# First image of an attention kernel's first phase: seven products for part of q and k and all of v, an early power on GpSimd, and a later place for the weights' sums

## The chip, the core and the metric

The kernel runs on one core of a Trainium2 chip. A core has TensorE (matmuls; PE in the profile, its weight loads PEld), VectorE (DVE), ScalarE (ACT), GpSimd (POOL) and SyncE (SP), each with its own queue of instructions that it takes in order. SP and ACT also start DMAs. Engines wait for one another through semaphores. Matmuls write to PSUM, of which there are eight banks; the other working memory is SBUF. The metric is the device time of one execution in microseconds (us), lower being better.

## The reference

Two attention layers run one after the other over x of shape (8, 512, 32, 32): eight images of 512 channels and 1024 tokens, in float32.

```python
# layer 0
h = group_norm(xf, gn_w, gn_b)                      # 32 groups of 16 channels, over all tokens
qkv = jnp.einsum('oc,bct->bot', qkv_w, h) + qkv_b[None, :, None]
qkv = qkv.reshape(b * NUM_HEADS, -1, T)             # 8 heads of 64 channels
q, k, v = jnp.split(qkv, 3, axis=1)
q = fake_quant(q); k = fake_quant(k); v = fake_quant(v)   # 8 bits, from the min and max of the whole tensor
w = softmax(jnp.einsum('bct,bcs->bts', q * scale, k * scale))
a = jnp.einsum('bts,bcs->bct', w, v)
x = xf + jnp.einsum('oc,bct->bot', proj_w, a) + proj_b[None, :, None]
# layer 1: group norm, one head of 512 channels, no quantization
x = x + proj(softmax(q k^T / sqrt(512)) v)
```

The minimum and maximum that `fake_quant` needs are taken over all eight images. So no score can be computed before q, k and v of all images are known.

## The kernel before

**Phases.** Phase 1 computes the norm and q, k and v of layer 0 for all images, keeps their running minima and maxima, and writes q, k and v to DRAM. It ends about 624 us into the span, where the next products (`fold`) start. Then the extremes are reduced over the core (a `partition_all_reduce` on GpSimd), and a long second phase reads q, k and v back, quantizes them, and does the attention of both layers. The change touches phase 1 alone, and in it the first image, image 0.

**How a product is tiled.** An image is a tile x of 128 partitions by 4 chunks of channels (cc) by 1024 tokens. Its norm is done in place. A q or k tile is 128 channels (two heads, j = 0 to 3) by 1024 tokens. Computed directly it takes two accumulators of 512 tokens with four matmuls each, one for each chunk (lines 643 to 646; matmuls are all recorded under line 192, the helper `mm`). A float32 matmul shows in the trace as two records.

**Seven products.** For images 1 to 7 q, k and v are computed by a scheme of the Strassen-Winograd kind: the product of 2 by 2 blocks takes seven block products rather than eight, at the cost of sums of blocks of the weights (`weight_sums`, once) and of the tokens (`token_sums`, for each image), and of extra additions when accumulators are read. `qk_block(b, j)` computes the q tile j and the k tile j together; `v_block(b, n)` computes a quarter of the tokens of each half for v. Each is a generator that stops after each of its seven products, and a caller takes turns between them. In a block, two accumulators x and y are written, read by VectorE or ScalarE, and written on: between two products into the same accumulator there is a reading that TensorE must wait for. Image 0 is computed directly, eight q and k tiles and eight v tiles, and the weights' sums are made meanwhile.

**Image 0.** Its norm is done chunk by chunk (`norm(0, CC)`), as the chunks of x arrive: statistics on VectorE, an average over groups by two tiny matmuls (`gps_a`, the second from `gd_a`), an addition on VectorE, the inverse square root as a power of -0.5 on GpSimd (line 246), and the scaling of the chunk on VectorE, in two halves of 512 tokens. The matmuls of the first two tiles (`early`) follow each chunk as it is ready. A library that the power needs is loaded by an instruction that stands in GpSimd's queue right behind the three `memset`s of lines 169 to 173. The constant part of each bias (`bias(i)`) comes from TensorE too: `wt`, then `wc` or `wr`.

**What sets the order.** The kernel is written in an order, and a scheduling layer puts the instructions of each engine in a sequence by priority and readiness; only the matmuls are chained to one another (in `mm`). The listing of the built program shows the result: on VectorE, the weights' sums (`wa` and `room`), which in the text come after image 0's norm, stand in the middle of the last chunk's norm, between its `gd_a` steps. On TensorE that chunk's `gps_a` stands ahead of one matmul of chunk 1 and four of chunk 2. The generators `ahead` (norm and sums of image 1) and `more` (the weights' sums) are advanced by hand between tiles.

**Buffers that matter.** Phase 1 has eight PSUM banks, three x buffers (so image 3 is loaded when image 0 is no longer read), four buffers for q and k tiles, three for v, and one each for the token sums of even and odd images.

Of the kernel before, what the change touches and what calls it, by code (L numbers as in the profile page):

```python
# [9 lines left out]
F32 = mybir.dt.float32  # L10
# [4 lines left out]
ALU = mybir.AluOpType  # L15
AX = mybir.AxisListType

P = 128
B, C, HH, WW = 8, 512, 32, 32
T = HH * WW  # L20
CC = C // P
NT = T // P
NH = T // 512
HEADS = 8
PAIRS = HEADS // 2
# [17 lines left out]
IN_ORDER = mybir.DependencyInfo(mybir.DependencyClass.NoSync, mybir.DependencyReason.DATA)  # L43
# [10 lines left out]
def attn_pair_kernel(  # L54
# [9 lines left out]
    nc = tc.nc  # L64
    PSUM = bass.MemoryType.PSUM

    class InOrder:
# [5 lines left out]

        def __init__(self, engine):
            self.engine, self.last, self.t, self.chores = engine, None, 0.0, []

        def __getattr__(self, name):
            op = getattr(self.engine, name)

            def call(*args, **kw):  # L80
                ins = op(*args, **kw).ins  # L81
                if InOrder.planned:
                    if name == "dma_start":
                        self.t = max(self.t, pe.t) + 0.5
                    if self.last is not None:
                        tc.add_manual_dep(ins, self.last.name, IN_ORDER, reason="order")
                    self.last = ins

            return call
# [52 lines left out]
    dve, act, pe = InOrder(nc.vector), InOrder(nc.scalar), InOrder(nc.tensor)  # L142
# [15 lines left out]
    const = ctx.enter_context(tc.tile_pool(name="const", bufs=1))  # L158
# [9 lines left out]
    fourth = const.tile([P, P], F32, name="fourth")  # L168
# [2 lines left out]
    nc.gpsimd.memset(ones16, 1.0)  # L171
    mhalf = const.tile([P, CC], F32, name="mhalf")
    nc.gpsimd.memset(mhalf, -0.5)


    gavg = const.tile([P, P], F32, name="gavg")
# [14 lines left out]
    def mm(ps, lhsT, rhs, **kw):  # L191
        ins = nc.tensor.matmul(ps, lhsT=lhsT, rhs=rhs, **kw).ins  # L192
        part = lhsT.shape[-1] / P if lhsT.shape[-1] in (32, 64) else 1.0
        if rhs.dtype in (BF, F16):
            part *= 0.25 * lhsT.shape[0] / P
        pe.t += math.prod(rhs.shape[1:]) * 1.677e-3 * part
        if last_mm[0] is not None:
            tc.add_manual_dep(ins, last_mm[0].name, IN_ORDER, reason="order")
        last_mm[0] = ins
# [71 lines left out]
    v_d = [dram.tile([P, NT, C], F32, tag=f"v{b}", name=f"v_d{b}") for b in range(B)]  # L271
# [8 lines left out]
    with ExitStack() as fast:  # L280
# [39 lines left out]
        cut, at = {}, 0  # L320
        for name, n in (
            ("qmax", N_MAX), ("kmax", N_MAX), ("vmax", NT * B), ("qmin", B * PAIRS),
            ("kmin", B * PAIRS), ("vmin", NT + (B - 1) * NT // 2),
        ):
            cut[name] = rcs[:, at : at + n]
            at += n
        qmax, kmax, vmax, qmin, kmin, vmin = cut.values()
# [37 lines left out]
        with tc.tile_pool(name="p1w", bufs=1) as p1w, tc.tile_pool(name="p1", bufs=3) as p1, tc.tile_pool(  # L365
            name="p1o", bufs=4
        ) as p1o, tc.tile_pool(name="ps_1", bufs=8, space=PSUM) as ps_1:

            def one(name):
                return ps_1.tile([P, 512], F32, tag="b", name=name)  # L370

            wqkv = p1w.tile([P, CC, 3 * C], F32, name="wqkv")
            wn = {}
            xs, hs, cs = {}, {}, {}
            col = {n: 0 for n in ("qmax", "kmax", "vmax", "vmin")}

            def column(name, tile_):
                col[name] += 1
                return tile_[:, col[name] - 1 : col[name]]
# [37 lines left out]
                for i in range(3)  # L417
            ] + [room[:, 4:6, :]]

            def weight_sums():  # L420
                tt = dve.tensor_tensor
                (a11, a12), (a21, a22) = (
                    [wqkv[:, k, bass.ts(i, C)] for k in (K0, K1)] for i in (0, 1)
                )
                tt(ss[0], a21, a22, ALU.add)
                yield
                tt(ss[1], ss[0], a11, ALU.subtract)
                yield
                tt(ss[2], a11, a21, ALU.subtract)
                yield  # L430
                tt(ss[3], a12, ss[1], ALU.subtract)
                yield
                (w11, w12), (w21, w22) = (
                    [wqkv[:, k, 2 * C + i * C // 2 : 2 * C + (i + 1) * C // 2] for i in (0, 1)]
                    for k in (K0, K1)
                )
                tt(vs[:, 0], w11, w12, ALU.subtract)
                yield
                tt(vs[:, 1], w22, vs[:, 0], ALU.subtract)
                yield  # L440
                tt(vs[:, 2], w22, w12, ALU.add)
                yield
                tt(vs[:, 3], w21, vs[:, 1], ALU.subtract)
                yield

            def quarters(b):
                h = hs[b]
                return [h[:, k, bass.ts(hf, 512)] for k in (K0, K1) for hf in range(NH)]

            def token_sums(b):  # L450
                a, b_, c, d = quarters(b)
                cs[b] = t = l1p.tile(
                    [P, 4, CC // 2, 512], F32, tag="hv"[b % 2], name=f"sums_{b}"
                )
                tt = dve.tensor_tensor
                tt(t[:, 0], b_, a, ALU.subtract)
                yield
                tt(t[:, 1], d, t[:, 0], ALU.subtract)
                yield
                tt(t[:, 2], d, b_, ALU.subtract)  # L460
                yield
                tt(t[:, 3], c, t[:, 1], ALU.subtract)
                yield
# [122 lines left out]
            vb = p1w.tile([P, 2, C], F32, name="vb")  # L586
# [37 lines left out]
            bq, bk, bv = (bias(i) for i in range(3))  # L624
            then = iter((part[1], part[2], part[2], part[3], part[3]))
            for cc in range(CC):
                for t in range(2):
                    for hf in range(NH):
                        qk_mm(0, early[t], t, hf, cc)
                        if (cc, hf) in ((0, 1), (1, 0), (1, 1)):  # L630
                            next(next(then, iter(())), None)
                if cc >= 2:
                    next(bq, None)
            load_x(2)
            ahead = prepare(1)
            more = weight_sums()
            hn = hs[0]
            for t in range(2 * PAIRS):
                isk, j = divmod(t, PAIRS)
                if t < 2:  # L640
                    ps = early[t]
                else:
                    ps = [one(f"qkps_0_{t}_{hf}") for hf in range(NH)]
                    for hf in range(NH):
                        for cc in range(CC):
                            qk_mm(0, ps, t, hf, cc)
                if t >= PAIRS - 1:
                    next(bk, None)
                if t == 2 * PAIRS - 1:
                    next(bv)  # L650
                qk = p1o.tile([P, T], F32, tag="qk", name=f"qk1_0_{t}")
                mx, mn = (kmax, kmin) if isk else (qmax, qmin)
                for hf in range(NH):
                    dve.tensor_scalar(
                        qk[:, bass.ts(hf, 512)], ps[hf], qkb[:, t : t + 1], None,
                        ALU.add, ALU.max, accum_out=column("kmax" if isk else "qmax", mx),
                    )
                dve.tensor_reduce(mn[:, j : j + 1], qk, AX.X, ALU.min)
                nc.sync.dma_start((k_d if isk else q_d)[0][j], qk)
                if t > 0:  # L660
                    next(ahead, None)
            for t in range(NT):
                ps = one(f"vps_0_{t}")
                for cc in range(CC):
                    mm(
                        ps,
                        lhsT=hn[:, cc, bass.ts(t, P)],
                        rhs=wqkv[:, cc, 2 * C : 3 * C],
                        start=(cc == 0),
                        stop=(cc == CC - 1),  # L670
                    )
                next(bv, None)
                vt = p1o.tile([P, 2, C], F32, tag="v2", bufs=3, name=f"v1_0_{t}")[:, 0, :]
                dve.tensor_add(vt, ps, vb[:, 0, :])
                dve.tensor_reduce(column("vmax", vmax), vt, AX.X, ALU.max)
                dve.tensor_reduce(column("vmin", vmin), vt, AX.X, ALU.min)
                nc.sync.dma_start(v_d[0][:, t, :], vt)
                next(ahead, None)
                next(more, None)
            for rest in (ahead, more):  # L680
                for _ in rest:
                    pass


            TURNS = (0, 0, 2, 0, 0, 2, 0, 2, 0, 0, 2, 1, 1, 2, 1, 1, 2, 1, 2, 1, 1)
            for b in range(1, B):
# [4 lines left out]
                ahead = prepare(b + 1) if b + 1 < B else iter(())  # L691
                for n in range(2):
                    blocks = (qk_block(b, 2 * n), qk_block(b, 2 * n + 1), v_block(b, n))
# [307 lines left out]
        xts, sums, wms, wps, mvs = {}, {}, {}, {}, {}  # L1001
# [62 lines left out]
        tt = dve.tensor_tensor  # L1064
# [924 lines left out]
```

## Time and profile before

| | us |
|---|---|
| median of 3 runs | 2689.42 |
| lowest and highest | 2688.77, 2689.55 |
| the profiled execution | 2690.02 |
| its span | 2688.2 |
| granted TensorE clock over the span | 0.99 |
| first matmul of q | at 14.40 |
| end of image 0's products | at 112.52 |
| end of image 1's products | at 185.6 |

Starts are counted from the span's start. "Busy" is the time in which an engine worked on instructions; the chain of waits is followed back from the last instruction, at each step to what released it. Of DMA, 10 MB arrive in the first 30 us (x of images 0 to 2 and the weights), at about 400 GB/s from 14 us on.

### The profile page before, as it was taken

The page shows a single profiled execution, that of the slowest core. Times are in us where ns is not written, and L with a number is a line of the kernel's source. Part 1 is how long each engine was busy: PE and PEld are TensorE (multiplying, and loading weights), DVE is VectorE, ACT ScalarE, POOL GpSimd, SP SyncE. Part 2 cuts the span into 40 slices and gives each one's busy share as a digit, 9 for nine tenths or more (in the row PEclk, how much of TensorE's full clock was granted, in tenths as well). Part 3 has the DMA queues.
Part 4 walks back from the last instruction along what each step waited for, and adds up shares of the span by engine and source line. Part 5 has one row for each costly group of instructions (what it writes and reads, how often), then busy time and mean ns, then how long its engine had stood idle before and what let it go on. Part 6 is the DMA issues. An engine that isn't in the chain of part 4 may idle for free.

```text
span 2688.2 us, 33380 instructions
## 1 busy us (share of the span) xinstructions
PE 2594.8 (97%) x13110; PEld 1657.8 (62%) x13110; DVE 1904.8 (71%) x2749; ACT 1259.0 (47%) x1582; POOL 201.7 (8%) x156
## 2 busy tenths in 40 slices
PE   7999999998779999999999999999999999999998
PEld 3455555553225774776577567757765775677687
DVE  6666666647997776876777687678767776876544
ACT  0011111114875665666476556646664765565021
POOL 0000000000220000100100010001001000100000
PEclk9999999998999999999999999999999999999999
DMA  5323223224421123212322321233133223212311
GB/s 196 113 110 125 101 96 117 94 113 146 134 64 40 56 68 118 95 56 94 111 64 71 107 87 56 79 109 94 56 95 110 64 76 103 87 40 69 112 36 37
DMA packets 147464, 241.97 MB, mean 90 GB/s; under 512 B 26592, under 2 KB 92128, under 8 KB 145760
## 3 DMA queue, kind: packets, MB, share of 16 engines
q1 hardware_dynamic: 116448, 181.50, 20.1%
q10 hardware_dynamic: 30848, 58.23, 6.3%
q8 instruction: 105, 1.72, 0.3%
q14 instruction: 63, 0.52, 0.1%
HBM read 152.86 MB, written 86.28 MB: 89 GB/s over the span
## 4 chain that ended last, share of the span: by engine, by line
PE 78%; DVE 9%; issue 7%; DMA 2%; ACT 2%; POOL 1%; SPq 0%; ACTq 0%; DVEq 0%; POOLq 0%
PE s L192 15%; PE o L192 13%; PE qkps L192 10%; PE pj L192 8%; PE av L192 7%; PE v2ps L192 7%; PE g L192 5%; PE vps L192 5%; PE st L192 4%; PE sm L192 4%; DVE two L81 2%; ACT pt L81 1%; DVE sums L81 1%; DVE x L81 1%; DVE h L81 1%
## 5 line engine op out<-in xcount | busy, mean ns | idle before, releaser
L81 DVE TENSOR_TENSOR two<-pt,two 128x1024 f16<-128x1024 f32 x512 | 618.1, 1225 | 165.9 <-POOL two L873 134.7
L81 ACT ACTIVATE pt<-st,esc 128x1024 f32<-128x1024 f32 x512 | 543.5, 1115 | 371.0 <-PE st L192 348.1
L81 ACT CAST two<-pt 128x1024 f16<-128x1024 f32 x364 | 369.5, 1055 | 7.8 <-ACT p L81 5.1
L873 POOL CAST two<-pt 128x1024 f16<-128x1024 f32 x128 | 177.1, 1384 | 1585.5 <-PE sm L192 1376.4
L81 ACT ACTIVATE u<-qkps,qkb 128x512 f32<-128x512 f32 x84 | 57.7, 687 | 476.5 <-PE qkps L192 472.1
L192 PE MATMUL av<-two,v 128*64 128x512 f16 x2048 | 255.3, 387 | 0.6
L192 PE MATMUL s<-g,h 128*128 128x256 f32 x1024 | 234.2, 381 | 0.0
L192 PE MATMUL pj<-ao,wp 128*128 128x512 f32 x512 | 223.9, 595 | 1.5 <-DVE ao L81 1.5
L192 PEld LDWEIGHTS s<-g,h 128*128 128x128 f32 x1024 | 192.9, 190 | 31.8 <-issue 4.3
L192 PE MATMUL st<-q,k 64*128 64x512 bf16 x1024 | 166.5, 386 | 42.3 <-ACT pt L81 35.6
L192 PEld LDWEIGHTS <-v 128*64 128x64 f16 x2048 | 104.1, 110 | 133.1 <-issue 62.0
L192 PE MATMUL s<-g,sums 128*128 128x256 f32 x768 | 178.4, 381 | 0.2 <-DVE p L81 0.2
L192 PE MATMUL o<-p,v 128*128 128x256 f32 x768 | 175.2, 382 | 0.0
L192 PEld LDWEIGHTS pj<-ao,wp 128*128 128x128 f32 x512 | 96.1, 190 | 123.1 <-issue 112.9
L192 PE MATMUL qkps<-x,wqkv 128*128 128x512 f32 x352 | 163.5, 608 | 1.8 <-DVE x L81 1.8
L192 PEld LDWEIGHTS o<-p,v 128*128 128x128 f32 x768 | 144.3, 190 | 25.6 <-issue 6.9
L192 PEld LDWEIGHTS s<-g,sums 128*128 128x128 f32 x768 | 144.7, 190 | 24.2 <-issue 4.6
L192 PE MATMUL qkps<-sums,wa 128*128 128x512 f32 x336 | 153.3, 592 | 0.0
L192 PE MATMUL sm<-two,ones 128*32 128x512 f16 x2048 | 141.6, 386 | 1.3 <-ACT rs L81 1.3
L192 PEld LDWEIGHTS <-k 64*128 64x128 bf16 x1024 | 36.6, 94 | 165.6 <-issue 163.1
L192 PE MATMUL o<-g,vsum 128*128 128x256 f32 x512 | 125.4, 401 | 11.5 <-DVE g L81 11.5
L192 PE MATMUL g<-h,wa 128*128 128x256 f32 x512 | 122.1, 387 | 2.5 <-DVE h L81 2.5
(193 smaller groups left out, 3504.8 us busy)
## 6 DMA issues: line engine op xcount, KB each, us to landing
rs<-rs_d SPq DMA_DIRECT2D x80, 256.0 KB
x<-in_x_dram SPq DMA_DIRECT2D x32, 512.0 KB
raw<-q_d SPq DMA_DIRECT2D x32, 512.0 KB
raw<-k_d SPq DMA_DIRECT2D x32, 512.0 KB
raw<-v_d SPq DMA_DIRECT2D x32, 512.0 KB
x_d<-h SPq DMA_DIRECT2D x64, 256.0 KB
x<-x_d ACTq DMA_DIRECT2D x64, 256.0 KB
out_dram<-x SPq DMA_DIRECT2D x64, 256.0 KB
```

Of the source, the lines that this page charges most:

```text
L81: ins = op(*args, **kw).ins
L192: ins = nc.tensor.matmul(ps, lhsT=lhsT, rhs=rhs, **kw).ins
L873: copy(two[:, 0], pt)
```

## The change

Four things are done.

- In image 0 the q and k tiles 0 and 1 are still computed directly (`for t in (0, 1, PAIRS, PAIRS + 1)`). The tiles 2 and 3 of q and k and all of v come from two rounds of a `qk_block` and a `v_block` taking turns, seven products each. The token sums of image 0 are made as well, and the order in which they and the weights' sums are advanced is written out.
- On GpSimd a power of constants, whose result nobody reads, stands behind the memsets. The library's load, which was followed by the first norm's power, now stands ahead of this one.
- Every sum of weights and of image 0's tokens is made to follow, on VectorE, the last instruction of the last chunk's norm (`tt_behind`, `dve.after(normed)`). This is an order only: both are on the same engine, and no semaphore is added.
- The biases of k and v are advanced earlier, and the columns of v's minima are counted anew.

```diff
 class InOrder
             self.engine, self.last, self.t, self.chores = engine, None, 0.0, []
+            self.latest = None
+
+        def after(self, ins):
+
+            tc.add_manual_dep(self.latest, ins.name, IN_ORDER, reason="order")
...
-                ins = op(*args, **kw).ins
+                ins = self.latest = op(*args, **kw).ins
...
     nc.gpsimd.memset(mhalf, -0.5)
+
+    nc.gpsimd.tensor_tensor(
+        const.tile([P, 1], F32, name="first_pow"), fourth[:, 0:1], mhalf[:, 0:1], ALU.pow
+    )
...
-            ("kmin", B * PAIRS), ("vmin", NT + (B - 1) * NT // 2),
+            ("kmin", B * PAIRS), ("vmin", B * NT // 2),
...
+            def tt_behind(*args):
+                dve.tensor_tensor(*args)
+                dve.after(normed)
+
             def weight_sums():
-                tt = dve.tensor_tensor
+                tt = tt_behind
...
 def token_sums(b)
-                tt = dve.tensor_tensor
+                tt = dve.tensor_tensor if b else tt_behind
...
                             next(next(then, iter(())), None)
+                            normed = dve.latest
...
             ahead = prepare(1)
-            more = weight_sums()
-            hn = hs[0]
-            for t in range(2 * PAIRS):
+            more, sums = weight_sums(), token_sums(0)
+
+            more = iter([more, more, sums, sums, more, more, more, more, sums, sums, more, more])
+            for t in (0, 1, PAIRS, PAIRS + 1):
...
-                if t >= PAIRS - 1:
+                if t == 1:
+                    next(bk)
+                elif t == PAIRS:
                     next(bk, None)
-                if t == 2 * PAIRS - 1:
                     next(bv)
+                elif t == PAIRS + 1:
+                    next(bv, None)
...
-                if t > 0:
-                    next(ahead, None)
-            for t in range(NT):
-                ps = one(f"vps_0_{t}")
-                for cc in range(CC):
-                    mm(
-                        ps,
-                        lhsT=hn[:, cc, bass.ts(t, P)],
-                        rhs=wqkv[:, cc, 2 * C : 3 * C],
-                        start=(cc == 0),
-                        stop=(cc == CC - 1),
-                    )
-                next(bv, None)
-                vt = p1o.tile([P, 2, C], F32, tag="v2", bufs=3, name=f"v1_0_{t}")[:, 0, :]
-                dve.tensor_add(vt, ps, vb[:, 0, :])
-                dve.tensor_reduce(column("vmax", vmax), vt, AX.X, ALU.max)
-                dve.tensor_reduce(column("vmin", vmin), vt, AX.X, ALU.min)
-                nc.sync.dma_start(v_d[0][:, t, :], vt)
-                next(ahead, None)
-                next(more, None)
-            for rest in (ahead, more):
-                for _ in rest:
-                    pass
+                for g in (next(more, None) for _ in range(2)):
+                    next(g)
+            for n in range(2):
+                blocks = (qk_block(0, 2 + n), v_block(0, n))
+                for i in range(14):
+                    next(blocks[i % 2])
+                    next(next(more, iter(())), None)
+                    if i % 2 == 1:
+                        next(ahead, None)
+            for _ in ahead:
+                pass
+            del hs[0], cs[0]
```

In the listing of the changed program, VectorE has the whole norm of the last chunk without a gap and then the sums of weights and tokens in turns; TensorE has k's tiles 0 and 1 behind q's, with the three biases between them, and then the 28 products; all instructions from image 1's first evictions on stand as before.

## The prediction, made before the changed kernel had run

> **What bounds the kernel now.** I read the page first, then the chain of waits over the first 180 us, then the busy time by stretches, then GpSimd's instructions in order of time.
>
> The page's first part says that TensorE is the bound:
> ```profile
> PE 2594.8 (97%) x13110; PEld 1657.8 (62%) x13110; DVE 1904.8 (71%) x2749; ACT 1259.0 (47%) x1582; POOL 201.7 (8%) x156
> ```
> The table by stretches (length, then busy PE, PEld, DVE, ACT, POOL, granted clock, DMA share, GB/s) says how full it is around the change. The first image's products end at 112.52 us:
> ```profile
> 28.00:30.00 2.00, 2.00 (x5) 0.80 (x4) 1.56 (x5) 0.00 (x0) 0.93 (x1) 0.68 0.56 219
> 30.00:32.00 2.00, 2.00 (x4) 0.91 (x3) 2.00 (x4) 0.00 (x0) 0.00 (x0) 0.50 0.00 0
> ...
> 36.00:112.52 76.52, 76.52 (x205) 34.29 (x204) 52.36 (x102) 1.17 (x2) 1.02 (x1) 1.00 0.25 96
> 112.52:185.60 73.08, 72.92 (x230) 42.91 (x229) 48.22 (x96) 8.24 (x12) 1.01 (x1) 1.00 0.28 106
> ```
> From 36 us on TensorE has no gap, while VectorE is busy 52 of 76 us: work taken from TensorE there moves everything after it. At 28 to 32 us TensorE looks full, but its clock was 0.68 and 0.50. The chain (start, length, what) shows what comes before that:
> ```profile
> 12.98 0.60 POOL grstd_a L246
> ...
> 13.60 0.16 DVE grstd_a L81
> ...
> 14.40 3.78 PE qkps L192 x4
> ...
> 24.81 1.05 issue
> 25.86 0.15 DVE gd_a L81
> 26.01 1.14 DVE wa L81
> 27.15 0.08 DVE gd_a L81
> 27.23 0.04 issue
> 27.27 0.38 PE gps_a L192 x2
> 27.65 6.10 PE qkps L192 x10
> ```
> Two 128x1024 sums of weights (wa; the "issue" of 1.05 us covers the first) stand on VectorE between the small steps (gd_a) of the last chunk's norm. TensorE, whose order puts that chunk's second average (gps_a) ahead of ten ready records, waits for it from 24.67 to 27.27. Then those ten records take 6.10 us.
>
> GpSimd and the step that releases it, from the order of time:
> ```profile
> 8.69 0.16 DVE L81 TENSOR_SCALAR grstd_a<-gps_a 128x1 f32<-128x1 f32 x1 [0.68 <-PE gps_a L192]
> 12.98 0.59 POOL L246 TENSOR_TENSOR grstd_a<-grstd_a,mhalf 128x1 f32<-128x1 f32 x1 [11.96 <-DVE gmv_a L81]
> 18.68 0.55 POOL L246 TENSOR_TENSOR grstd_a<-grstd_a,mhalf 128x1 f32<-128x1 f32 x1 [5.11 <-DVE grstd_a L81]
> ...
> 823.18 1.04 POOL L873 CAST two<-pt 128x1024 f16<-128x1024 f32 x1 [17.42 <-PE sm L192]
> 831.89 1.05 POOL L246 TENSOR_TENSOR grstd_b<-grstd_b,mhalf 128x4 f32<-128x4 f32 x1 [7.67 <-issue]
> ```
> The first power's input is ready at 8.85, yet it starts at 12.98; the second starts 0.08 after its input.
>
> [...] after the 2.60 us gap, records that otherwise step 0.43 us stepped 0.86 until about 32 us. [...] Here 7.67 us pass before the power at 831.89, whose library is reloaded behind the cast. But the all-reduce at 626.79, also after a reload, came 0.14 us after its input, having been queued for over 100 us: the load seems paid where the reload stands, not at the first call. [...] The last chunk's power took 0.93 us beside two-input sums, and 0.55 without.
>
> **The change, part by part.**
>
> *Weights' sums behind the last norm.* VectorE's new order has the norm of chunk 3 without a gap and all sums after it. Chunk 2 shows its price: from its first gd_a at 21.69 to its average's start at 22.24 is 0.55. Chunk 3's first gd_a stands at 24.59, so TensorE resumes at 25.14, not 27.27: 2.13 us. The idle gap falls to some 0.5 us[...]: ten records at 0.43 are 4.29, not 6.10, 1.81 us more (bounds 0 and 1.81). The chunk is ready about 27.6; its matmuls come after the ten records and the bias's wt, at about 31: not late.
>
> *Fewer products.* Removed: q and k tiles 2, 3, 6 and 7 (in the chain 13.84 + 6.97 + 6.97 = 27.78) and v (3.63 + 24.03 = 27.66), in all 55.44. Added: 14 q/k products (two matmuls of 512 columns) at 1.72 and 14 v products (four of 256) at 1.73, as image 1's rows in the chain have them: 24.08 + 24.22 = 48.30. Saved 7.14, less 0.09 since the second k tile now follows a bias too (7.06 against 6.97): 7.05. The bias sums and image 1's two averages stay, only earlier.
>
> *What they cost VectorE.* From the last norm to the end of the first image, by start-to-start steps: sums of weights 4 x 1.14 + 4 x 0.60 = 7.0; tokens of images 0 and 1, 8 x 1.14 = 9.1 (half of it new); four direct tiles, two evictions at 0.67 and a minimum of 1.13 each, 9.9; the blocks, 14 x 0.61 + 2 x 0.67 + 6 x 0.60 + 8 x 1.13 = 22.5; statistics of images 1 and 2, 15 x 0.60 + 0.8 = 9.8; image 1's norm 4.2; v's bias 1.2: 64 us in 75. So it has room in sum. In order: the sums are first read by the blocks' third products, about 60 us; the eight long sums and two short ones end about 42, the last two short ones about 50. Each block's accumulators rest while the other block multiplies. The tightest I find is the third reading of v's first accumulator, queued behind k's eviction, which waits for ScalarE's u4 (0.69): about 1.05 us before TensorE returns to it. Banks of the early tiles are needed at 46 and read by 38. I cost waits at nothing; if that cover goes, each product is late by what VectorE is late. ScalarE's six added evictions (0.69 each) stand in an idle queue.
>
> *DMA.* Eight v stores of 256 KB become four of 512; q and k keep eight. Image 3's load waits, as before, for image 0's last reader. On SP its last three chunks stand behind the last v store, ready some 1.9 us after the handover (before 0.76), so land about a microsecond later; their statistics now stand further back too. Nothing.
>
> *The constants' power.* The trace does not show it, and the reload stands right behind the memsets in both programs, without a wait. If the load runs from there (1.02 to 12.98), the new power starts at 12.98 and the real one 0.55 later: a loss of 0.55, since everything to 24.7 us is a chain through it. If the load is paid at the first call, it is done by then; VectorE still waits for chunk 1's DMA (10.44), its statistics (11.99) and its average (12.63), so the first x comes at 12.82 instead of 13.81: a gain of 0.99. The all-reduce speaks for the first; I take the loss of 0.55.
>
> **Sum.** 2.13 + 1.81 + 7.05 - 0.55 = 10.44 us. The profiled execution took 2690.02 (span 2688.2 and 1.8 around it): 2679.6 in its terms. The median shown is 0.60 below it: 2679.0. Later images and the second layer keep their orders and have TensorE as their bound, so they start earlier and nothing is given back.
>
> **Rivals.** *The load is paid at the first call*: 1.54 better, 2677.4. For it: 4.1 us from release to start, near the 4.7 from release (827.2) at 831.89. Against it: the all-reduce. *The head stays ragged*: the clock falls again (1.81) or single products wait, up to 5 us: 2681 to 2684. [...] *VectorE sets the pace*: if the two blocks do not cover each other and each of the 28 products waits for one eviction of 0.69, 19.3 us come back and the time is 2698.3, slower. It is a loss from 0.37 us a product (10.4 / 28). For it: VectorE at 85% with minima of 1.13 standing ahead of evictions. Against it: image 1 runs such blocks with three in turn and VectorE at 48 of 73 us, and TensorE lost only 0.16 there. *Half of that*, 6 to 10 us lost: no change that can be told.
>
> **Chances.** Forecast 0.60, load at the first call 0.17, ragged head 0.12, no change 0.06, VectorE's pace 0.05. About 0.2% (5.4 us) is what a measurement here can tell from no change; the first three make faster 0.89. The range runs from below the second case to most of the third, 2676.3 to 2683.0; it leaves out the last two and a little of the third.
>
> **What would show it.** Right: no gap of over 1 us in TensorE at 24 to 28 us and a clock of 1.00 at 28 to 32; image 0's products end near 102.1 (25.69 + 27.86 of head, biases and direct tiles + 48.5) instead of 112.5; a first power at about 13.0 and the real one at 13.5. Wrong: a first power before 9 us (second case), gaps before v's or k's products released by VectorE, or an end that moved less than the 112.52.

## The result, and the profile after

| | before | after |
|---|---|---|
| median, us | 2689.21 (7 runs) | 2677.68 (7 runs) |
| lowest and highest, us | 2685.17, 2690.08 | 2674.34, 2680.66 |
| ratio, 95% interval | | 0.9959, 0.9950 to 0.9968 |
| profiled execution, us (span) | 2690.02 (2688.2) | 2674.34 (2672.5) |
| last chunk's second average starts, us | 27.27 | 23.90 |
| image 0's products end, us | 112.52 | 100.51 |
| all-reduce of the extremes starts, us | 626.79 | 615.15 |

The changed kernel is faster by 11.0 us (8.6 to 13.4 by the interval of the ratio). The forecast was 2679.0 in a range of 2676.3 to 2683.0. The two profiled executions lie 15.7 us apart, more than the medians: the one of after happens to be the fastest of its seven. So its end is not read against the forecast. What is read is the stretch up to the all-reduce, where the change acts.

First, the page's busy times of after. TensorE is still the bound, with 12.2 us less of work than before and a few more instructions:
```profile
PE 2582.6 (97%) x13150; PEld 1663.0 (62%) x13150; DVE 1909.5 (71%) x2755; ACT 1263.1 (47%) x1588; POOL 204.1 (8%) x157
```
The chain of waits of after through the head and to the end of image 0's products (start, length, what):
```profile
1.08 10.42 issue
11.50 0.59 POOL first_pow L180
12.09 0.54 POOL grstd_a L255
...
13.46 3.56 PE qkps L201 x4
...
20.96 0.40 PE gps_a L201 x2
...
23.53 0.14 DVE gd_a L86
23.66 0.02 issue
23.69 0.17 DVE gd_a L86
23.86 0.04 issue
23.90 0.38 PE gps_a L201 x2
24.29 4.40 PE qkps L201 x10
...
98.79 1.73 PE vps L201 x8
100.51 3.43 PE qkps L201 x8
```
No sum stands between the `gd_a` steps any more. The average starts at 23.90, and the ten records behind it take 4.40 us, not 6.10. The record at 100.51 is image 1's first. The power on constants starts behind GpSimd's 10.42 us of "issue", and the real power directly behind it.

The table by stretches of after (length, then busy PE, PEld, DVE, ACT, POOL with counts, granted clock, DMA share, GB/s):
```profile
28.00:30.00 2.00, 2.00 (x11) 0.46 (x10) 2.00 (x3) 0.23 (x1) 0.00 (x0) 1.00 0.52 207
30.00:32.00 2.00, 2.00 (x6) 0.90 (x5) 2.00 (x3) 0.36 (x1) 0.00 (x0) 1.00 0.00 0
...
60.00:80.00 20.00, 20.00 (x75) 13.62 (x74) 15.14 (x36) 2.06 (x3) 1.02 (x1) 1.00 0.25 97
80.00:101.00 21.00, 21.00 (x74) 13.88 (x73) 16.78 (x29) 1.37 (x2) 0.00 (x0) 1.00 0.16 64
```
The clock is 1.00 where it was 0.68 and 0.50, and through the 28 products (from 51.86 us on) TensorE has no gap, with VectorE at 32 of the last 41 us.

**How a run is taken apart.** Three distances along the chain are used for every run below. "Real power" is the start of the first power that the norm needs. The *lead* is from there to the last chunk's second average (`gps_a`). The *stage* is from that average to the end of image 0's products. Before: 12.98, 14.29, 85.25. After: 12.08, 11.82, 76.61. From the end of image 0 to the all-reduce it is 514.25 to 514.32 us in ten of the eleven profiles of this study (514.64 in the first one of after, which lost 0.36 around image 4). So what the head gains reaches the all-reduce whole. From the all-reduce to the end of the span it was 2061.4 before and 2057.4 to 2062.5 in the others. That varies by 5 us between kernels whose second phase is the same (e7 and e9, which add a little to it, lie within), and it is 4.0 of the 15.7 us between the two profiles.

The lead also holds parts that the sums' order does not touch, above all TensorE's first four records, which took from 3.41 (e1, e2) to 3.78 us (before, e3, e5, e8) with no link to the edits. So a shorter stretch is read beside it, from chunk 2's second average to chunk 3's. Before, the first of the two is
```profile
22.24 0.40 PE gps_a L192 x2
```
and the stretch is 27.27 - 22.24 = 5.03 us. It is 4.68 in e2, and 2.94 or 2.95 in after, e1, e3, e4, e5, e7 and e8.

### The profile page after: what moved, and what is told of

It reads as the page before. It is cut to its first block, busy times and chain, and to the rows that moved or that the text cites. A ratio compares the mean times of both kernels' runs of the same rounds, so it can differ in the third digit from the quotient of the medians.

```text
span 2672.5 us, 33466 instructions
## 1 busy us (share of the span) xinstructions
PE 2582.6 (97%) x13150; PEld 1663.0 (62%) x13150; DVE 1909.5 (71%) x2755; ACT 1263.1 (47%) x1588; POOL 204.1 (8%) x157
## 3 DMA queue, kind: packets, MB, share of 16 engines
q8 instruction: 105, 1.72, 0.3%
## 4 chain that ended last, share of the span: by engine, by line
PE 80%; DVE 8%; issue 7%; ACT 2%; DMA 1%; POOL 1%; ACTq 0%; SPq 0%; DVEq 0%; POOLq 0%
PE s L201 15%; PE o L201 14%; PE qkps L201 10%; PE pj L201 8%; PE av L201 7%; PE v2ps L201 7%; PE g L201 6%; PE vps L201 5%; PE st L201 4%; PE sm L201 4%; DVE two L86 2%; ACT pt L86 1%; DVE sums L86 1%; DVE x L86 1%; DVE h L86 1%
## 5 line engine op out<-in xcount | busy, mean ns | idle before, releaser
L201 PE MATMUL qkps<-sums,wa 128*128 128x512 f32 x360 | 164.9, 592 | 0.1
L201 PE MATMUL qkps<-x,wqkv 128*128 128x512 f32 x304 | 140.8, 602 | 1.3 <-DVE x L86 1.3
L201 PE MATMUL o<-g,vsum 128*128 128x256 f32 x512 | 123.7, 397 | 11.5 <-DVE g L86 11.5
```

## The experiments

All ran beside the kernel before on the same chip: the first four (before 2687.8 us, 37 runs), the next four (2687.6, 15 runs) and the last alone (2687.84, 10 runs). All lines from the trace are in us.

| run | real power | lead | stage | all-reduce | median us (runs) | ratio, 95% |
|---|---|---|---|---|---|---|
| before | 12.98 | 14.29 | 85.25 | 626.79 | 2689.21 (7) | |
| after | 12.08 | 11.82 | 76.61 | 615.15 | 2677.68 (7) | 0.9959 (0.9950 to 0.9968) |
| e1, no power on constants | 12.87 | 11.72 | 76.61 | 615.48 | 2678.12 (6) | 0.9965 (0.9953 to 0.9977) |
| e2, sums where they fall | 12.66 | 14.48 | 78.30 | 619.71 | 2682.22 (15) | 0.9980 (0.9973 to 0.9988) |
| e3, only the sums' order | 11.69 | 12.37 | 83.55 | 621.88 | 2685.89 (13) | 0.9990 (0.9982 to 0.9998) |
| e4, v directly | 14.09 | 11.95 | 81.21 | 621.54 | 2682.29 (14) | 0.9976 (0.9968 to 0.9984) |
| e5, block after block | 14.39 | 12.14 | 80.65 | 621.50 | 2682.51 (10) | 0.9978 (0.9969 to 0.9987) |
| e6, no first root | none | | 76.61 | 613.16 | 2674.87 (1) | |
| e7, root on ScalarE | none | | 76.61 | 615.00 | 2679.43 (6) | 0.9971 (0.9959 to 0.9983) |
| e8, after again | 12.23 | 12.15 | 76.61 | 615.27 | 2677.57 (5) | 0.9961 (0.9948 to 0.9975) |
| e9, first chunk first | none | | 76.61 | 613.49 | 2679.98 (6) | 0.9971 (0.9959 to 0.9983) |

The theory is the prediction's sum: the sums' order is worth a shorter wait and a clock that stays at 1.00, the products their shorter matmuls, the power on constants nothing or a small loss, and VectorE's readings no wait. The rivals are its own: the load is paid at the first call; VectorE sets the pace.

### e3: only the sums' order, added to the kernel before

```diff
 class InOrder (of the kernel before)
+        def after(self, ins):
+            tc.add_manual_dep(self.latest, ins.name, IN_ORDER, reason="order")
...
 def weight_sums()
-                tt = dve.tensor_tensor
+                tt = tt_behind
```

> The kernel before with that order alone: direct products, no early power. Theory: the gap of 2.60 us falls to about 0.5 and the clock stays at 1.00 from 28 to 32 us: 3 to 4.5 us below the kernel before, image 0's products ending near 108.5. Rival (TensorE only waits elsewhere): under 1 us.

The chain of e3:
```profile
21.11 0.40 PE gps_a L196 x2
...
24.06 0.38 PE gps_a L196 x2
24.44 4.40 PE qkps L196 x10
```
The stretch between the two averages is 2.08 us shorter than before, and the stage 1.70, which is just the ten records (4.40 against 6.10). Together 3.78, inside the 3 to 4.5 that the theory gave. The lead as a whole shows only 1.92 of the 2.08: the power came so early here that the first x waited for VectorE's work on the second chunk instead. At the all-reduce it is 4.91, because the real power also happened to come 1.29 earlier. In timed runs the gain is 2.7 us (0.5 to 4.8), which agrees without adding to it.

### e2: the change without that order

```diff
             def tt_behind(*args):
                 dve.tensor_tensor(*args)
-                dve.after(normed)
```

> The changed kernel without the order that puts the sums behind the last norm; the listing has the weights' sums between the steps of the last two chunks' norms again. Theory (the order is worth 2.1 us of waiting and up to 1.8 us of clock): TensorE's gap ahead of the last chunk's average is 2 us or more again, and image 0's products end 2 to 4 us later than in the changed kernel: 7.5 to 9.5 us below the kernel before. Rival (seven products alone carry the gain, and the gap is refilled later): as fast as the changed kernel, 11 to 12 us below.

The chain of e2 in the norm of chunks 2 and 3, and its stretch at 24 us:
```profile
21.01 1.13 DVE sums L86
22.14 0.08 DVE gd_a L86
...
22.46 0.40 PE gps_a L201 x2
...
23.11 1.47 POOL grstd_a L255
...
25.88 1.14 DVE wa L86
27.02 0.08 DVE gd_a L86
...
27.14 0.59 PE gps_a L201 x2
27.73 5.88 PE qkps L201 x10
```
```profile
24.00:28.00 4.00, 2.71 (x5) 1.14 (x6) 3.56 (x10) 0.00 (x0) 0.57 (x1) 0.50 1.03 410
28.00:30.00 2.00, 2.00 (x3) 0.74 (x3) 1.54 (x4) 0.00 (x0) 1.57 (x1) 0.50 0.56 225
```
Now a sum of tokens stands in the norm of chunk 2, and sums of weights in that of chunk 3. Against e8, chunk 2's average comes 1.1 us later for the token sum. From it to chunk 3's average is 1.73 us more (4.68), and 0.91 of that is GpSimd's power: it took 1.47 us while VectorE ran a sum of weights, and 0.56 in e8. The stage is 1.69 longer. Together that is 4.5 us, over the 2 to 4 that were expected; the difference in the table is 4.02 (2.33 in the lead, 1.69 in the stage) because TensorE's first four records and the average behind them happened to take 0.47 us less here than in e8. In the timed runs e2 is 4.6 us slower than the two series of after, and 5.4 (3.2 to 7.3) below before, where 7.5 to 9.5 were expected. The rival, that the products alone carry the gain, is excluded. So the order is worth 4.5 us inside the change and 3.8 alone: without it the new token sum adds its own harm to that of the weights' sums.

The clock is 0.50 through 24 to 30 us. By the trace it fell at 23.8 us, behind a gap of 1.99 us (to 22.46) and before the next, of 1.29 (to 27.14). Before, it fell at 28.7, behind a gap of 2.60. Gaps of 0.92 and 0.51 in after brought no fall. Nor did longer ones earlier in the head, of 3.40 us before (to 12.05) and 2.81 in after (to 11.57). At 0.50 it stayed for 3.4 us before (28.7 to 32.1) and 6.8 in e2 (23.8 to 30.6). What decides when it falls, and for how long, these runs don't settle.

### e4: v of image 0 directly, between the q and k products

```diff
-                blocks = (qk_block(0, 2 + n), v_block(0, n))
-                for i in range(14):
-                    next(blocks[i % 2])
+                block = qk_block(0, 2 + n)
+                for i in range(7):
+                    next(block)
...
+                    if i % 2 == 0:
+                        t = 4 * n + i // 2
+                        ps = one(f"vps_0_{t}")
+                        for cc in range(CC):
+                            mm(ps, lhsT=hs[0][:, cc, bass.ts(t, P)], rhs=wqkv[:, cc, 2 * C : 3 * C],
+                               start=(cc == 0), stop=(cc == CC - 1))
...
```

> The changed kernel with v of image 0 computed directly again (eight tiles, put between the products of the q and k block); q and k stay. Theory (the gain of the products is TensorE's own time): 27.5 against 24.2 us of v products, so image 0 ends 3.2 to 3.5 us later than in the changed kernel, 7.5 to 9 us below the kernel before. Rival (VectorE sets the pace in the blocks, so lighter work on it gains back): under 1.5 us later, or earlier.

The stage is 4.60 us longer than after, where 3.2 to 3.5 were expected. Counting tiles gives 8 x 3.44 - 14 x 1.73 = 3.3; the chain of e4 shows what came on top:
```profile
69.45 3.45 PE vps L201 x8
...
72.92 0.69 DVE v L86
73.61 0.07 DVE gd_a L86
73.67 1.25 DVE rcs L86 x2
74.92 0.07 DVE gmean_a L86
74.99 0.07 DVE gd_a L86
75.06 0.67 DVE q L86 x2
75.73 0.09 DVE gd_a L86
...
75.86 0.39 PE gps_a L201 x2
```
TensorE's queue has image 1's second average (`gps_a`) here, and VectorE has two reductions of v (`rcs`) and an eviction of q between the small steps (`gd_a`) that release it. TensorE waits 1.04 us, the only such gap, and the average itself takes 0.39 us where after has 0.12. With the 3.3 of the products that makes the 4.60. VectorE had stood idle for 1.95 us just ahead of the eviction of v, so this is its order and not its load: the same pattern as the weights' sums in the head. The forecast's "no wait on VectorE" thus holds for this change's order and not for every arrangement of image 0. In the timed runs e4 is 4.7 us slower than the two series of after; its gain over before, 6.5 us (4.3 to 8.6), is below the 7.5 to 9 that were expected.

### e5: the blocks one after another

```diff
-                    next(blocks[i % 2])
+                    next(blocks[i // 7])
```

> The changed kernel with one edit: in the first image each block's seven products run without the other block's between them (all seven of q/k, then all seven of v, twice). Same products, same sums, same instructions on VectorE. Theory (a product waits only where its accumulator was written by the product just before it): in a block the fifth and the sixth product go into the same accumulator, and its reading (0.69 us on ScalarE or VectorE) is then not covered: four places in TensorE's chain, each with a wait of 0.7 to 1.0 us, 3 to 4 us in all, image 0's stage (from the last chunk's average to the end of its products) 79.5 to 80.6 us instead of 76.6, time 2680 to 2682. Rival (VectorE sets the pace once the blocks do not cover each other): a wait at nearly every one of the 28 products, up to 0.69 each, 10 to 19 us, stage 87 to 96, time 2688 or more. Second rival (the order makes no difference, VectorE's readings are always in time): stage 76.6, no wait, time 2677 to 2678.

What TensorE waited for between 40 and 110 us in e5 (total, times, longest), and the first of these places in its chain:
```profile
PE qkps L201 <- ACT u L86: 1.6, 2, 0.8
PE vps L201 <- DVE uv L86: 1.4, 2, 0.8
```
```profile
54.49 8.60 PE qkps L201 x20
...
63.17 0.70 ACT u L86
63.87 0.04 issue
63.91 3.70 PE qkps L201 x8
```
Four waits, one in each block, where the fifth and the sixth product go into one accumulator; 3.0 us of waiting, and the records behind each take some 0.27 more (3.70 for eight of q and k, 3.43 without a wait). The stage is 4.04 us longer, the timed runs 4.9 us slower than e8. That is the theory (3 to 4, and four places), a little over its upper end, as is the time (2682.51, where 2680 to 2682 were expected). The rival's 10 to 19 us did not come, even without the other block as cover: VectorE kept up with products of 1.72 us. What the turns buy is only the place where an accumulator is written twice running.

### e1, e6, e7, e8: the power on constants and the load

e1 takes the power on constants away. e6 does so too, and leaves out the square root of image 0's first chunk (a reciprocal instead), so that GpSimd is first asked at the second chunk. e7 keeps the root, by ScalarE's square root and VectorE's reciprocal. e8 is the changed kernel again.

```diff
 e1, e6 and e7
-    nc.gpsimd.tensor_tensor(
-        const.tile([P, 1], F32, name="first_pow"), fourth[:, 0:1], mhalf[:, 0:1], ALU.pow
-    )
...
 e6
-        nc.gpsimd.tensor_tensor(rstd, rstd, mhalf[:, 0:n], ALU.pow)
+        if nm == "a0_0":
+            dve.reciprocal(rstd, rstd)
+        else:
+            nc.gpsimd.tensor_tensor(rstd, rstd, mhalf[:, 0:n], ALU.pow)
...
 e7
+        if nm == "a0_0":
+            act.activation(rstd, rstd, AF.Sqrt)
+            dve.reciprocal(rstd, rstd)
+        else:
+            nc.gpsimd.tensor_tensor(rstd, rstd, mhalf[:, 0:n], ALU.pow)
```

> The changed kernel without the power of constants. If the library's load runs from where the reload stands (my theory), the first norm's power comes 10 to 12 us after the reload, with nothing between, and chunk 0 is scaled about 0.55 us earlier for the same length of load: 11 to 13 us below the kernel before, not to be told from the changed kernel. If the load is paid at the first call (rival), the first norm's power starts about 4 us after its input, and the kernel is some 1.5 us slower than the changed one: 9 to 10.5 us below the kernel before.

> The changed kernel without the power on constants, and with the first chunk's power in the first image replaced by a reciprocal on VectorE: it leaves out that chunk's square root, so this part of the result is another number, at the same cost in the later stages. GpSimd's first power is then that of the second chunk, whose input is ready no earlier than about 17 us. Theory (the load starts at the reload near 1.0 us and ends by itself 10.5 to 12.5 us later): GpSimd's second-chunk power starts within 0.1 us of its input, at about 16 to 18 us. Rival (the load is paid when a power is first asked for): it starts 4 us or more after its input, at 21 us or later. In both: the first chunk's x is no longer behind the load but behind the second chunk's statistics, 0 to 1.3 us earlier.

> The changed kernel without the power on constants, and with the first chunk's power in the first image done by ScalarE's square root and VectorE's reciprocal: the same result by another way. Theory (the first chunk's x waits for GpSimd's load, up to about 12 to 13.5 us, and without it waits for VectorE's work on the second chunk, to about 12.0 to 12.8): the last chunk's average starts 0 to 1.5 us earlier than the 23.90 to 26.04 of the runs with a power, never later than 24.6, image 0's products end near 99.5 to 101, time 2676.5 to 2678, not told apart from the changed kernel. Rival (ScalarE's own table load for the square root, some 1.3 us each, stands in the way of the sums of rows that ScalarE copies): image 0's stage grows by 1 to 2.6 us, time 2679 to 2681.

> The changed kernel once more, for the spread of one kernel between executions and on the same chip as the others of this group. Theory (the load at the head differs from one execution to the next and everything in the first image follows it): the first power anywhere from 11.5 to 13.5 us, the last chunk's average 10.8 to 12.6 us after the real power, image 0's stage 76.6 us within 0.1, time 2676 to 2680. Rival (the 11.50 of the first profile belongs to this kernel, because the power stands earlier in the queue): the first power at 11.5 within 0.1 again.

GpSimd's first powers in order of time; e1, then e8:
```profile
12.87 0.59 POOL L251 TENSOR_TENSOR grstd_a<-grstd_a,mhalf 128x1 f32<-128x1 f32 x1 [11.85 <-issue]
```
```profile
11.65 0.59 POOL L180 TENSOR_TENSOR first_pow<-fourth,mhalf 128x1 f32<-128x1 f32 x1 [10.63 <-issue]
12.23 0.54 POOL L255 TENSOR_TENSOR grstd_a<-grstd_a,mhalf 128x1 f32<-128x1 f32 x1
```
and e6, with the VectorE step that releases the power:
```profile
16.38 0.16 DVE L86 TENSOR_SCALAR grstd_a<-gps_a 128x1 f32<-128x1 f32 x1 [2.06 <-PE gps_a L197]
```
```profile
16.70 0.60 POOL L254 TENSOR_TENSOR grstd_a<-grstd_a,mhalf 128x1 f32<-128x1 f32 x1 [15.68 <-DVE grstd_a L86]
```
e6 decides: no power had its input before 16.54 us, and the power came 0.16 after it (in e7 also 0.16, at 17.59), where the theory had 0.1 and the rival 4 or more. So the load was over by itself, in e6 and e7 before the first call could run. No profile has a record of the load. Its start is taken from the program, where the reload stands right behind the memsets (these end at 1.0 us), and its end from a first power that waits for no input, as after's does behind 10.42 us of "issue". In e2, e4, e5, after and e8 a power without any input to wait for, standing right behind it, did not make it end sooner (it started from 11.50 to 13.81; without it the first power came from 11.69 to 12.98, in before, e1 and e3).

e1 alone decides nothing. Its first power, at 12.87, is 11.8 us after the reload, as the theory has it, and 4.0 after its input, as the rival has it. Its gain over before in timed runs, 9.4 us (6.2 to 12.6), is below the 11 to 13 of the theory and in the range of the rival (9 to 10.5).

So the power on constants can only do what the forecast said: occupy GpSimd for 0.58 us once the load is over, with the real power behind it. Whether that shows depends on the load. The first power of any kind started at 11.50 (after), 11.65 (e8), 11.69 (e3), 12.08 (e2), 12.87 (e1), 12.98 (before), 13.52 (e4) and 13.81 (e5), so the time from the reload at 1.0 varies from 10.5 to 12.8 us, with the same instructions ahead of it. The rival of e8, an early 11.5 that belongs to this kernel, falls: e4 and e5 have the same power and started at 13.52 and 13.81. (In e8 itself it was 11.65, which alone would not have told.) What makes the load longer or shorter was not tried. The times of e1 and after, 0.4 us apart, cannot show 0.58.

e7 shows a floor under the head: with no power in the way its first x starts at 12.85, because VectorE's order has the second chunk's statistics (from 10.32) and average ahead of that x. Counted from these statistics the floor is 2.53 us, and by that measure, an estimate, x could have started at 12.5 in after and 12.6 in e8 (statistics at 9.99 and 10.03) instead of 12.87 and 13.02. So where the load ends early, the power on constants costs some 0.3 to 0.5 us rather than the whole 0.58. e6 agrees that it is the order: there VectorE happened to have the first x (at 11.77) ahead of the second chunk's average, and it has the earliest all-reduce of all, 613.16.

e7's all-reduce comes at 615.00, against 615.15 and 615.27. Its time, 2679.43 us, is over the 2676.5 to 2678 expected and in the range of its rival, ScalarE's table. The rival's reason is not seen in image 0, whose stage is 76.61. But the table does cost something, further on. ScalarE in e7 behind the all-reduce, then in e8:
```profile
627.39 1.28 ACT L86 ACT_TABLE_LOAD   x1
628.69 2.12 ACT L86 ACTIVATE pt<-st,esc 128x1024 f32<-128x1024 f32 x2
```
```profile
627.53 2.13 ACT L86 ACTIVATE pt<-st,esc 128x1024 f32<-128x1024 f32 x2
```
Before, after and e7 have a table load of 1.28 us at 2.13 us. e7 and e9, the two with a root on ScalarE, have a second one, right ahead of the second phase's first exponentials (`pt`), where before, after and e8 have none. The exponentials start 12.26 us after the all-reduce in before and e8, 12.27 in after, 13.69 in e7 and 13.68 in e9.

### e9: a faster head, not seen in the time

e7, with the first chunk's norm emitted first and its x put ahead of the second chunk's statistics.

```diff
-            for g in (*part, part[0], part[0], part[1]):
+            for g in (part[0], part[0], part[0], *part[1:], part[1]):
...
                     dve.bn_stats(st[:, i, hf, :], src(cc, hf))
+                    if nm == "a0_1":
+                        dve.after(normed0[0])
```

> The kernel with the root of the first chunk on ScalarE (no power on constants), and the first chunk's x put ahead of the second chunk's statistics on VectorE. Same results. Theory (with the load out of its way, the head is set by VectorE, whose order has the second chunk's statistics and averages before the first x at 12.85): the first x starts at 10.0 to 10.4 us, the last chunk's average at 21.5 to 23.0 instead of 24.14, image 0's stage stays 76.6, the all-reduce comes at 612.3 to 613.9 instead of 615.0, and the time is 1 to 2.6 us less, 2675 to 2677.5, hardly told apart from the changed kernel by its time. Rival (the later chunks' loads set the head): the first x is early but the last chunk's average stays at 23.9 to 24.4, all-reduce at 614.8 to 615.3, time 2677 to 2679.

The chain of e9:
```profile
10.10 1.00 DVE x L86 x2
...
22.62 0.38 PE gps_a L197 x2
23.01 4.40 PE qkps L197 x10
```
Up to the all-reduce the theory holds: x at 10.10, the average at 22.62 (24.14 in e7), the all-reduce at 613.49 (615.00). That is 1.5 us by the trace. The time does not follow: 2675 to 2677.5 was expected, the median is 2679.98 us, not below after's. The second table load of 1.28 us stands here too, at 625.88, and sets the second phase's first exponentials back by 1.4 us against e8, about what the head had won. The expectation had left it out. Whether it lasts to the end is not shown, since the rest of the second phase varies by more. The intervals of the two ratios overlap, so these runs neither show the 1.5 us nor exclude them; no version is shown to beat the changed kernel.

## Why the prediction was right

**Sums behind the last norm, 2.13: right.** From chunk 2's average to chunk 3's it fell from 5.03 to 2.94 us in after, 2.09 less, and by as much in e3 and e8. (The leads as a whole fell by 2.14 in e8, 2.47 in after and 1.92 in e3, for the reasons given above.) The average's idle wait is 0.51 us in after, about the 0.5 that was expected. The forecast did not price one thing that the order also spares: GpSimd's power took 0.93 to 1.57 us beside VectorE's sums and 0.55 without.

**Clock, 1.81: right, by 0.11 too large.** The ten records went from 6.10 to 4.40, so 1.70, both in after and in e3. With a gap of 0.51 us the clock stayed at 1.00, as forecast. That a fall goes with the length of the gap was the author's estimate, from before's gap of 2.60, and is not shown: in e2 the clock fell behind one of 1.99, and before's gap of 3.40 earlier in the head brought no fall.

**Products, 7.05: right, 6.94.** TensorE's work in the stages of e3 and after differs by nothing else: 83.55 - 76.61.

**No waits on VectorE: right for this order.** In after and e8 no gap in the 28 products, and no product that waits. The covers were real: e5 takes one of them away in each block, and each uncovered place costs about 1.0 us. The rival of 19.3 us had taken a wait for each product; in e5 only the second of two products in turn on one accumulator waited. The one wait of e4 (1.04) is for the steps of image 1's norm, not for an accumulator.

**The power on constants, a loss of 0.55: right in kind.** The real power stands 0.58 behind it, and the load is not paid at the first call (in e6 and e7 the first power came 0.16 us after its input). That the head loses all of it is shown by no pair of runs: where the load ended early (after, e8) VectorE's order would have taken up part of it. The load's own variation of 2.3 us is larger. The forecast took the 12.98 of one profile as the load's end: it said a first power at about 13.0 and a real one at 13.5, and the profile of after has 11.50 and 12.08. That term makes image 0 end at 100.51 instead of the 102.1 of the forecast. It is luck of that execution and no effect of an edit. With the load of before put in, the measured parts give 12.98 + 0.58 + 12.15 + 76.61 = 102.3.

**The sum, 10.44.** Measured in e8's terms: 2.14 + 8.64 - 0.58 = 10.20, before what the load happens to do. The timed gain is 11.0 us in the first series and 10.5 (6.7 to 14.0) in e8's. The shift reached the all-reduce undiminished, as said: 514.3 us from image 0's end in nearly every profile. Beyond it the second phase's own 5 us hide whether it stays whole; the timed gains agree with it.

**The rivals.** The load paid at the first call (2677.4) lies closer than the forecast to the median of 2677.68, and its mechanism is wrong all the same: e6 and e7 exclude it. A forecast can be near for a wrong reason, since a load that ends 1 us earlier by chance moves the head just as that rival would.

## What to carry over

Before pricing a stage that is full on the bound engine, look at the head that feeds it: two sums of 1.1 us between the small steps of a norm cost here 3.8 us (e3), over half of what 28 shorter products saved, because the clock also fell to 0.50 behind the wait of 2.60 us. To judge whether accumulators that are read and written again will stall, look for two products in a row into the same one; those needed other work between them here (0.7 to 0.8 us of waiting each without it, in e5), and the rest had their cover in the next product's own 1.72 us. And when runs of one kernel differ by 5 us, take a 2 us effect apart between fixed points of the trace (one average to the next, image 0's end to the all-reduce), where the same parts mostly agreed to 0.1 us, rather than by the ends. Where a function moves to another engine, look for what that engine then loads later on (here a second table load of 1.28 us, in e7 and e9).

## What was not expected of the hardware

- GpSimd's first power started from 10.5 to 12.8 us after the memsets' end at 1.0 us (at 11.50 in after, 13.81 in e5) in eight profiles with the same instructions before it; the load that this time is put down to has no record of its own.
- A power of 128x1 took 0.55 us alone and 1.46 and 1.57 beside two-input sums on VectorE (e2); before showed 0.93.
- TensorE's clock fell to 0.50 behind gaps of 2.60 us (before) and 1.99 (e2), and stayed there for 3.4 and 6.8 us. Gaps of 3.40 (before) and 2.81 (after) earlier in the head brought no fall.
- The second phase, with the same instructions (but for the table load of 1.28 us of e7 and e9), lasted from 2057.4 to 2062.5 us after the all-reduce.
